# Ordering the last expert blocks by row, results in rows per batch row, and a combine beside them

## The chip, the cores and the metric

The kernel runs on one core of one Trainium2 chip. The metric is the device time of one execution in microseconds (us), as the median of several runs. All data are 32-bit floats.

## The reference

There are B = 4 rows of T = 512 tokens with C = 512 channels. Each row goes through two layers. In each of the four parts a gate computed from side inputs and from x itself comes first, and the part's result is added to x.

```python
x = x + mamba2(gate(x, ...), ...)                 # layer 0, state space model (SSM)
x = x + experts(gate(x, ...), gate_w, gate_b, w1, b1, w2, b2)
x = x + attention(gate(x, ...), w_q, w_kv, w_dense)   # causal, 16 heads, 4 groups
x = x + ffn(gate(x, ...), ...)

def gate(r, k, v, w, u, time_emb):       # scans over the tokens, both ways
    ...
    base = sigmoid(r) * (num / maximum(den, 1e-08))
    return base * (0.8 + 0.2 * tf)

def experts(hidden, ...):                # 8 experts, the best 2 for each token
    logits = x @ gate_w.T + gate_b
    top_vals, top_idx = top_k(logits, 2)
    routing = softmax(top_vals)
    for e in range(8):
        h = x @ w1[e].T + b1[e]
        y = h[:, 0::2] * sigmoid(1.702 * h[:, 0::2]) * (h[:, 1::2] + 1.0)
        ye = y @ w2[e].T + b2[e]
        out = out + ye * sum(routing * (top_idx == e))
```

The change lies in the experts' part and at its border to the attention. Only `sigmoid(r)` of a gate depends on x; the scans, `num` and `den` do not, and are made beside other work.

## The kernel before, in words

**Experts.** Each token has two picks, so there are 4096 picks. They are sorted by expert into blocks of P = 128, where a block holds one expert's picks only; NBLK = 39 blocks always suffice, and those at the end that no pick needs run as dummies. The gated activations of all tokens lie in DRAM as `rows_h`, one row for each token (stored in `logits`, L486). A block gathers its 128 rows with an indirect DMA on POOL (`fetch`, L683, three ahead), turns them with four transposes (`flip`, pfl L695, copied to hT by ACT L697), and runs one round:

- `first_half`: the product pg with the gate half of w1 (L724), g on DVE (L729), a tanh on ACT; then the product pn with the linear half (L735) and two DVE steps to u (L742).
- `finish`: u is turned by four transposes, pyt (L748), and scaled into yT by ACT (L750).
- `down`: the product po with w2 (L757), o on DVE (L762), and an indirect DMA on POOL (L763) that scatters the 128 rows of o into `rows_o`, one row for each pick.

In `round()` for block i, in program order: pg of i, po of i-2, the turn pfl of i+1, pn of i, and `finish` of i-1. The scheduler of the language decides the order on each engine from this, and may move an instruction ahead of others; `after(engine)` (L83) forbids what stands under it to be placed before the last instruction that the engine has so far.

**Two parts.** The first NEARLY = 17 blocks hold picks of rows 0 to 2 and run beside the SSM of row 3. When row 3 is routed (`route` L488: counts by matmuls pcnt, offsets on DVE L553, token numbers by ptok L555), `order_blocks(NEARLY, NBLK)` (L588) ranks the blocks that are left, by a matmul with a lower triangle (pidx L603), and makes for each place the list of rows to gather (`idx_h`), of rows to scatter to (`idx_o`) and its expert (`eb`). The id of a pick (`res_id`, L436) is its row in `rows_o`: 1 + 2048 for a second pick + the token's number over all rows; row 0 is for dummies. idx_h comes from it by an addition and a mask. The blocks stand in the order of the experts, whatever their row.

Weights go on SP's queue (`weights`, `load_w1` L657, `load_w2` L668). The first 17 blocks have one slot of weights; from block 17 on there are two, taken in turn, and a slot is loaded only when its expert changes.

**Border to the attention.** `combine(b)` (L1351) takes a row's results back: for each of four tiles of 128 tokens two loads of 128 x 512 on SP's queue (rr L1359), a scaling on ACT (L1361), a scaled sum on DVE (L1362), four transposes on PE (pcb L1367) and an addition to x on DVE (L1371). A load must come after every scatter to `rows_o` that could touch the same rows, and a scatter can touch all of them. Then `gated` loads what is made of the gate for the attention (1 MB, SP), takes tanh of x on ACT and multiplies on DVE. The attention starts with the keys pk (L1435) and values pv (L1443) of row 0, group 0. Rows 1 to 3 are combined beside the heads of the row before.

The gates' scans and divisions, which need no x, are a generator that `pump()` takes one step at a time; `more()` (L1378) does so after every round. The two parts meet here:

```python
        order_blocks(NEARLY, NBLK)
        moe.know(NBLK)
        more(NBLK - 8)
        first_group = load_group(0)
        more(NBLK)
        moe.round()
        moe.round()
```

Of the kernel before, what the change touches and what calls it, by code (L numbers as in the profile page):

```python
# [31 lines left out]
TOPK = 2  # L32
# [4 lines left out]
NROW = B * T * TOPK + 1  # L37

NEARLY = -(-((B - 1) * T * TOPK - E * (P - 1)) // P)

HEADS, GROUPS, KVC = 16, 4, 128
HPG = HEADS // GROUPS
# [36 lines left out]
def block_kernel(ctx: ExitStack, tc: tile.TileContext, a: dict, out: bass.AP):  # L79
# [61 lines left out]
    def ps_tp(name):  # L141
        return ps.tile([P, 512], F32, tag="tp", name=name, bufs=2)
# [316 lines left out]
    def logits(h, b, lg, t0, nt):  # L459

        pl = ps_tp("pl")
        for t in range(nt):
            for k in range(NC):
                nc.tensor.matmul(
                    pl[:, t * E : (t + 1) * E],
                    lhsT=h[:, k, t * P : (t + 1) * P],
                    rhs=gw[:, k, :],
                    start=(k == 0),
                    stop=(k == NC - 1),
                )  # L470
        nc.vector.tensor_tensor(
            lg[:, t0 : t0 + nt, :],
            pl[:, : nt * E].rearrange("p (t e) -> p t e", e=E),
            row("gate_b").unsqueeze(1).to_broadcast([P, nt, E]),
            ALU.add,
        )
        for t in range(nt):
            ph_ = ps_tp("pht")
            for k in range(NC):
                nc.tensor.transpose(  # L480
                    ph_[:, k * P : (k + 1) * P], h[:, k, t * P : (t + 1) * P], ident
                )
# [107 lines left out]
    def order_blocks(lo, hi):  # L590

        n = hi - lo
        cv = rt.tile([P, 1], F32, tag="cv", name="cv")
        nc.vector.tensor_tensor(jk, sel, cnt[:, (N2 if lo else N2 - NT), :], ALU.mult)
        nc.vector.tensor_reduce(cv, jk, AX.X, ALU.add)
        use = rt.tile([P, 1], F32, tag="use", name="use")
        if lo == 0:
            nc.vector.scalar_tensor_tensor(use, v_lo, float(P), cv, ALU.add, ALU.is_le)
        else:
            nc.vector.tensor_tensor(use, v_lo, cv, ALU.is_lt)  # L600
            nc.vector.tensor_tensor(use, use, taken, ALU.subtract)
        pi = ps_tp("pidx")
        nc.tensor.matmul(pi[:, P : P + 1], lhsT=tri_lt, rhs=use, start=True, stop=True)  # L603
        rank = rt.tile([P, 1], F32, tag="vrank", name="vrank")
        nc.vector.tensor_copy(rank, pi[:, P : P + 1])
# [8 lines left out]
        nc.vector.tensor_scalar(gf[:, :n], pi[:, :n], B * T - 1.0, None, ALU.add)  # L614
        nc.vector.tensor_copy(idx_h[:, lo:hi], gf[:, :n])
        nc.vector.tensor_scalar(idx_h[:, lo:hi], idx_h[:, lo:hi], B * T - 1, None, ALU.bitwise_and)
        ef = tmp.tile([1, NBLK], F32, tag="th", name="ef")
        nc.vector.tensor_scalar(ef[:, :n], pi[0:1, 2 * P : 2 * P + n], E - 1.0, None, ALU.add)
        nc.vector.tensor_copy(eb[:, lo:hi], ef[:, :n])
        nc.vector.tensor_copy(idx_o[:, lo:hi], pi[:, :n])  # L620

    class Experts:
# [130 lines left out]
        def down(self, i):  # L753
            s, yT = self.reg[i][0], self.yT.pop(i)
            po = ps_acc("po")
            for j in range(NI):
                nc.tensor.matmul(  # L757
                    po, lhsT=yT[:, j, :], rhs=self.w2[s][:, j, :],
                    start=(j == 0), stop=(j == NI - 1)
                )  # L760
# [16 lines left out]
        def round(self):  # L777
# [558 lines left out]
    def load_group(g):  # L1336
# [11 lines left out]
            )  # L1348
        return wq, wkv

    def combine(b):  # L1351

        for t in range(NT):
            bt = b * NT + t
            rr = []
            for c in range(2):
                r = cb.tile([P, C], F32, tag=f"rr{c}", name=f"rr{c}", bufs=2 - c)
                lo = 1 + c * B * T + bt * P
                nc.sync.dma_start(out=r, in_=rows_o[lo : lo + P, :])  # L1359
                rr.append(r)  # L1360
            nc.scalar.mul(rr[0], rr[0], g1[:, bt : bt + 1])  # L1361
            nc.vector.scalar_tensor_tensor(  # L1362
                rr[0], rr[1], g2[:, bt : bt + 1], rr[0], ALU.mult, ALU.add
            )
            pt = ps_tp("pcb")
            for k in range(NC):
                nc.tensor.transpose(  # L1367
                    pt[:, k * P : (k + 1) * P], rr[0][:, k * P : (k + 1) * P], ident
                )
            xs = x[b][:, :, t * P : (t + 1) * P]  # L1370
            nc.vector.tensor_tensor(xs, xs, pt.rearrange("p (k t) -> p k t", t=P), ALU.add)  # L1371

    with tc.tile_pool(name="moe_w2", bufs=1, reuse_waits="tile") as wm:
        moe.add_slot(wm)
# [26 lines left out]
    with att as ph:  # L1401
# [15 lines left out]
            )  # L1417
            return wd

        hs = [None] * B  # L1420

        class Group:
            pass
# [255 lines left out]
```

## Time and profile before

| | us |
| --- | --- |
| runs | 2666.9, 2674.48, 2674.92 |
| median | 2674.48 |
| the profiled execution, own time | 2663.89 |
| its span on the core | 2662.2 |
| mean granted TensorE clock | 0.978 |

The profile names five engines: PE (matmul), PEld (its weight loads), DVE (vector), ACT (scalar), POOL and SP (here they mainly issue DMAs). By stretches of the span, busy time in us and the DMA engines' mean share:

| stretch | what runs | PE | DVE | ACT | POOL | clock | DMA |
| --- | --- | --- | --- | --- | --- | --- | --- |
| 500 to 830 | SSM of row 3, experts' first blocks beside it | 311.9 | 199.9 | 131.6 | 80.8 | 0.95 | 0.26 |
| 830 to 960 | last of the first 17 blocks, counting of row 3 | 120.3 | 68.1 | 38.8 | 22.3 | 0.99 | 0.52 |
| 960 to 1215 | blocks 17 to 38 | 250.2 | 148.5 | 79.0 | 44.2 | 1.00 | 0.83 |
| 1215 to 1260 | combine of row 0, its gate | 14.7 | 11.8 | 8.4 | 1.0 | 0.62 | 0.62 |
| 1260 to 1900 | attention | 620.8 | 375.2 | 302.2 | 0.0 | 0.99 | 0.15 |

A busy time close to the stretch's length says that the engine has no gaps there; PE is that engine nearly everywhere, except from 1215 to 1260. The last scatter is issued at 1219.77 and lands at 1222.94; the first result tile is asked for at 1223.59, and pk starts at 1251.0. The granted clock is that of PE, 1 being full speed.

### The profile page before, as it was taken

The numbers are of one execution on the slowest core, as the hardware profiler recorded it, in microseconds if no ns is written. First come the engines' busy times: TensorE is split into PE (matmuls) and PEld (weight loads), VectorE is DVE, ScalarE is ACT, GpSimd is POOL, SyncE is SP. The second block draws the span as 40 slices with busy tenths as digits, with TensorE's granted clock in tenths as the row PEclk, the third lists the DMA queues.
The fourth block names the chain that finished last, engine by engine and source line by source line (L and its number), as shares of the span: only waits on it lengthen the run. The fifth ranks groups of instructions, "written<-read, shape, count | busy, mean of one in ns | idle before, by whom it ended". The sixth has DMA issues, their size and how long they took to land.

```text
span 2662.2 us, 24889 instructions
## 1 busy us (share of the span) xinstructions
PE 2505.3 (94%) x8398; PEld 1330.1 (50%) x8398; DVE 1432.2 (54%) x2777; ACT 1003.3 (38%) x2044; POOL 284.7 (11%) x403
## 2 busy tenths in 40 slices
PE   3999999999998999995999999999999999999999
PEld 1555555646644444442555555555555554444444
DVE  8888888886524565553675555555454441010110
ACT  4556646455321233331554544444444341000000
POOL 1141322322311111110000000000000000000000
PEclk9989999899998999997999999999999999999999
DMA  6121412213134487875121201111000003000000
GB/s 211 44 70 56 133 44 83 92 56 127 41 128 168 170 313 301 333 303 191 56 87 28 63 29 36 44 44 32 16 9 33 23 27 120 16 0 16 8 8 16
DMA packets 86111, 237.95 MB, mean 89 GB/s; under 512 B 9184, under 2 KB 18528, under 8 KB 75872
## 3 DMA queue, kind: packets, MB, share of 16 engines
q1 hardware_dynamic: 77440, 211.71, 22.9%
q0 software_dynamic: 6240, 20.45, 2.1%
q10 hardware_dynamic: 2304, 4.20, 0.4%
q8 instruction: 67, 1.10, 0.2%
q14 instruction: 60, 0.49, 0.1%
HBM read 268.05 MB, written 46.92 MB: 118 GB/s over the span
## 4 chain that ended last, share of the span: by engine, by line
PE 46%; DVE 4%; ACT 2%; DMA 1%; issue 1%; SPq 0%; POOLq 0%; ACTq 0%; DVEq 0%
PE pd L1521 8%; PE pq L1457 7%; PE pfu L1588 6%; PE pfo L1598 6%; PE pfg L1583 6%; PE pctx L1506 5%; PE psc L1474 3%; PE pv L1443 2%; PE ptp L1497 2%; PE pk L1435 2%; DMA rr<-rows_o 1%; DVE nmax L1479 1%; ACT pr L1484 1%; DVE psc L1477 0%; DVE den L260 0%
## 5 line engine op out<-in xcount | busy, mean ns | idle before, releaser
L1457 PE MATMUL pq<-h,wq 128*128 128x512 f32 x512 | 248.9, 603 | 7.5 <-ACT pr L1484 7.4
L1521 PE MATMUL pd<-cx,wd 128*128 128x512 f32 x512 | 222.4, 593 | 0.0
L923 PE MATMUL pc<-h,wxb 128*128 128x512 f32 x320 | 143.2, 605 | 38.1 <-DVE h L1199 38.1
L1593 DVE SCALAR_TENSOR_TENSOR hd<-pfu,cols,hd 128x512 f32<-128x512 f32 x44 | 33.1, 751 | 269.3 <-PE pfu L1588 269.2
L1592 ACT ACTIVATE hd<-pfg,cols 128x512 f32<-128x512 f32 x44 | 30.2, 687 | 381.0 <-PE pfg L1583 381.0
L1484 ACT ACTIVATE pr<-psc,nmax 128x128 f32<-128x128 f32 (+3 forms) x256 | 135.1, 529 | 98.2 <-DVE nmax L1479 97.3
L1477 DVE TENSOR_TENSOR psc<-psc,mask 128x128 f32<-128x128 f32 x256 | 71.9, 288 | 186.2 <-PE psc L1474 186.2
L1506 PE MATMUL pctx<-pT,v 128*128 128x512 f32 (+3 forms) x512 | 153.4, 443 | 7.3 <-ACT pT L1500 3.9
L1588 PE MATMUL pfu<-h,ffu 128*128 128x512 f32 x352 | 158.7, 593 | 1.0 <-DMA ffu<-in_upT 1.0
L1583 PE MATMUL pfg<-h,ffg 128*128 128x512 f32 x352 | 158.6, 593 | 0.0
L1521 PEld LDWEIGHTS pd<-cx,wd 128*128 128x128 f32 x512 | 96.2, 190 | 114.6 <-issue 110.6
L1474 PE MATMUL psc<-kT,qT 128*128 128x128 f32 (+3 forms) x512 | 151.4, 435 | 0.9 <-ACT pr L1484 0.7
L1598 PE MATMUL pfo<-hd,ffd 128*128 128x512 f32 x352 | 151.7, 592 | 0.0
L724 PE MATMUL pg<-w,hT 128*128 128x512 f32 x312 | 143.7, 602 | 2.0 <-DMA w<-in_w1x 2.0
L757 PE MATMUL po<-w,yT 128*128 128x512 f32 x312 | 142.5, 598 | 2.7 <-ACT yT L750 2.1
L1506 PEld LDWEIGHTS pctx<-pT,v 128*128 128x128 f32 x512 | 93.7, 191 | 97.5 <-issue 35.8
L735 PE MATMUL pn<-w,hT 128*128 128x512 f32 x312 | 140.3, 593 | 0.0
L1529 DVE TENSOR_TENSOR xr<-xr,pd 128x512 f32<-128x512 f32 x64 | 44.0, 688 | 175.5 <-PE pd L1521 175.5
L1479 DVE TENSOR_REDUCE nmax<-psc 128x1 f32<-128x128 f32 (+3 forms) x256 | 123.8, 486 | 2.7
L1457 PEld LDWEIGHTS pq<-h,wq 128*128 128x128 f32 x512 | 87.8, 193 | 65.9 <-issue 57.4
L1497 PEld LDWEIGHTS ptp<-ident,pr 128*128 128x128 f32 x640 | 77.3, 142 | 85.3 <-issue 39.0
L994 PE MATMUL pz<-wzt,h 128*128 128x512 f32 x256 | 119.1, 606 | 0.0
(292 smaller groups left out, 4297.6 us busy)
## 6 DMA issues: line engine op xcount, KB each, us to landing
w<-in_w1x SPq DMA_DIRECT2D x80, 1024.0 KB
w<-in_w2x SPq DMA_DIRECT2D x40, 1024.0 KB
wb<-in_b1x SPq DMA_DIRECT2D x40, 512.0 KB
kt<-in_fT SPq DMA_DIRECT2D x62, 256.0 KB
ek<-ek SPq DMA_DIRECT2D x62, 256.0 KB
ekv<-ekv SPq DMA_DIRECT2D x62, 256.0 KB
g<-num SPq DMA_DIRECT2D x30, 512.0 KB
h<-g SPq DMA_DIRECT2D x11, 1024.0 KB
```

The source lines that it names most:

```text
L724: nc.tensor.matmul(pg, lhsT=hT[:, k, :], rhs=self.w1[s][0][:, k, :], start=(k == 0), stop=(k == NC - 1))
L757: nc.tensor.matmul(po, lhsT=yT[:, j, :], rhs=self.w2[s][:, j, :], start=(j == 0), stop=(j == NI - 1))
L923: nc.tensor.matmul(pc, lhsT=wxb[:, k, m * P : (m + 1) * P], rhs=h[:, k, :], start=(k == 0), stop=(k == NC - 1),)
L1457: nc.tensor.matmul(pq, lhsT=u.wq[:, k, i * KVC : (i + 1) * KVC], rhs=u.h[:, k, :], start=(k == 0), stop=(k == NC - 1),)
L1474: nc.tensor.matmul(psc[:, :n], lhsT=qT[:, qi * P : n], rhs=u.kT[:, :n], start=True, stop=True)
L1479: nc.vector.tensor_reduce(nmax, psc[:, :n], AX.X, ALU.max, negate=True)
L1484: nc.scalar.activation(pr, psc[:, :n], AF.Exp, bias=nmax, accum_out=rsum)
L1506: nc.tensor.matmul(pctx[:, kj * P :], lhsT=u.v[:, kj, :], rhs=pT[:, kj, kj * P :], start=(kj == 0), stop=(kj == NT - 1),)
L1521: nc.tensor.matmul(po, lhsT=u.wd[:, i, m * P : (m + 1) * P], rhs=u.ctxT[i], start=(i == 0), stop=(i == HPG - 1),)
L1583: nc.tensor.matmul(pg, lhsT=wg[:, k, cs], rhs=h[:, k, :], start=(k == 0), stop=(k == NC - 1))
L1588: nc.tensor.matmul(pu, lhsT=wu[:, k, cs], rhs=h[:, k, :], start=(k == 0), stop=(k == NC - 1))
L1598: nc.tensor.matmul(po, lhsT=wdn[:, i, m * P : (m + 1) * P], rhs=hd[i], start=(i == 0), stop=(i == NFF - 1),)
```

## The change

The change has four pieces.

- **Rows of their own.** The ids of the picks are arranged so that each row of the batch has 1024 result rows in one piece: rows 3, 1, 2, 0 of the batch in this order (`AT`), so row 0's results are the last 1024 of `rows_o`. `rows_h` takes the same order of rows, and `idx_h` comes from the id by a mask, a shift and two exclusive ors.
- **Order of the last blocks.** Among the blocks from 17 on, those with picks of row 0 come first, each kind still in the order of experts. At most FIRST = 15 blocks can be of the first kind, so from block 32 on no block holds a pick of row 0, and its scatter is given `rows_o` without the last 1024 rows.
- **Combine of row 0 beside the last blocks.** `combine` is split into `load_results` and `add_results`. Row 0's results are loaded on POOL's queue from block 34's round on, and added tile by tile between the rounds of the last blocks; so is the gate of row 0 (`early_h`, held in a tile of wq's), ahead of the last two `down`. A copy of it for the other groups is made by a DMA on SP.
- **`finish` under `after(nc.tensor)`**: pyt of block i-1 may no longer be placed ahead of pn of block i.

```diff
+FIRST = (T * TOPK + E * (P - 1)) // P
...
+    AT = (TOPK * T) * np.array([B - 1, *range(1, B - 1), 0])
...
-    res_id = [count(f"res{c}", [[P, B * NT]], 1, 1 + c * B * T) for c in range(2)]
+    res_id = [count(f"res{c}", [[TOPK * T, B], [P, NT]], 1, 1 + c * T) for c in range(2)]
+    for r in res_id:
+        for b in (0, B - 1):
+            rb = r[:, b * NT : (b + 1) * NT]
+            nc.vector.tensor_scalar(rb, rb, float(AT[b] - b * TOPK * T), None, ALU.add)
...
-            lo = b * T + (t0 + t) * P
+            lo = (B - 1) * T - int(AT[b]) // TOPK + (t0 + t) * P
...
+        else:
+
+            two = rt.tile([P, 2], F32, tag="two", name="two")
+            nc.vector.tensor_tensor(jk, sel, cnt[:, NT, :], ALU.mult)
+            nc.vector.tensor_reduce(rank, jk, AX.X, ALU.add)
+            nc.vector.tensor_scalar(two[:, 0:1], v_lo, rank, use, ALU.is_lt, ALU.mult)
+            nc.vector.tensor_tensor(two[:, 1:2], use, two[:, 0:1], ALU.subtract)
+            nc.tensor.matmul(pi[:, P : P + 2], lhsT=tri_lt, rhs=two, start=True, stop=True)
+            nc.tensor.matmul(pi[:, P + 2 : P + 3], lhsT=ones, rhs=two[:, 0:1], start=True, stop=True)
...
-        nc.vector.tensor_scalar(idx_h[:, lo:hi], idx_h[:, lo:hi], B * T - 1, None, ALU.bitwise_and)
+        low = tmp.tile([P, NBLK], I32, tag="th", name="low")
+        nc.vector.tensor_scalar(
+            low[:, :n], idx_h[:, lo:hi], T - 1, (B - 1) * T, ALU.bitwise_and, ALU.bitwise_xor
+        )
+        nc.vector.tensor_scalar(
+            idx_h[:, lo:hi], idx_h[:, lo:hi], 1, (B - 1) * T,
+            ALU.logical_shift_right, ALU.bitwise_and,
+        )
+        nc.vector.tensor_tensor(idx_h[:, lo:hi], idx_h[:, lo:hi], low[:, :n], ALU.bitwise_xor)
...
-                out=rows_o[:, :],
+                out=rows_o[: NROW - (TOPK * T if i >= NEARLY + FIRST else 0), :],
...
-                self.yT[i - 1] = self.finish(self.y.pop(i - 1))
+                with after(nc.tensor):
+                    self.yT[i - 1] = self.finish(self.y.pop(i - 1))
...
+    def load_results(b, t, queue):
+
+        rr = []
+        for c in range(2):
+            r = cb.tile([P, C], F32, tag=f"rr{c}", name=f"rr{c}", bufs=2)
+            lo = 1 + int(AT[b]) + c * T + t * P
+            queue.dma_start(out=r, in_=rows_o[lo : lo + P, :])
+            rr.append(r)
+        return rr
...
     def combine(b):
 
         for t in range(NT):
...
+            add_results(b, t, load_results(b, t, nc.sync))
...
         first_group = load_group(0)
-        more(NBLK)
+
+        more(min(NEARLY + FIRST + 2, NBLK - NT - 1))
+        results = {t: load_results(0, t, nc.gpsimd) for t in range(2)}
+        more(moe.i + 1)
+        for t in range(NT):
+            more(moe.i + 1)
+            with after(nc.tensor, nc.vector, nc.scalar):
+                add_results(0, t, results.pop(t))
+            if t + 2 < NT:
+                results[t + 2] = load_results(0, t + 2, nc.gpsimd)
+        assert moe.i == NBLK
+        early_h = gated(2, 0, x[0], wa, tag="wq", name="h2_0")
         moe.round()
         moe.round()
...
-        hs = [None] * B
+        hs = [gp.tile([P, NC, T], F32, tag="h", name="h2")] + [None] * (B - 1)
+        nc.sync.dma_start(out=hs[0], in_=early_h)
...
-            if g == 0 and b == 0:
-                combine(b)
-                hs[b] = gated(2, b, x[b], gp, tag="h", name=f"h2_{b}")
-            u.h = h = hs[b]
+            u.h = h = early_h if (g, b) == (0, 0) else hs[b]
```

`add_results` holds the four steps of the old `combine` behind its loads, unchanged. In `order_blocks` the rank of a block of the second kind is its count among its kind plus the number of those of the first kind; the first call, for the 17 early blocks, ranks as before.

More of the change, by code (lines that the diff above doesn't have):

```diff
@@ L602, in order_blocks @@
         pi = ps_tp("pidx")
-        nc.tensor.matmul(pi[:, P : P + 1], lhsT=tri_lt, rhs=use, start=True, stop=True)
         rank = rt.tile([P, 1], F32, tag="vrank", name="vrank")
-        nc.vector.tensor_copy(rank, pi[:, P : P + 1])
+        if lo == 0:
+            nc.tensor.matmul(pi[:, P : P + 1], lhsT=tri_lt, rhs=use, start=True, stop=True)
+            nc.vector.tensor_copy(rank, pi[:, P : P + 1])
+        else:
[7 more added lines that the diff above has]
+            nc.vector.tensor_scalar(
+                rank, pi[:, P + 1 : P + 2], pi[:, P + 2 : P + 3], two[:, 1:2], ALU.add, ALU.mult
+            )
+            nc.vector.scalar_tensor_tensor(
+                rank, pi[:, P : P + 1], two[:, 0:1], rank, ALU.mult, ALU.add
+            )
         if lo == 0:
@@ L613, in order_blocks @@
         gf = tmp.tile([P, NBLK], F32, tag="th", name="gf")
-        nc.vector.tensor_scalar(gf[:, :n], pi[:, :n], B * T - 1.0, None, ALU.add)
+        nc.vector.tensor_scalar(gf[:, :n], pi[:, :n], NROW - 2.0, None, ALU.add)
         nc.vector.tensor_copy(idx_h[:, lo:hi], gf[:, :n])
-        nc.vector.tensor_scalar(idx_h[:, lo:hi], idx_h[:, lo:hi], B * T - 1, None, ALU.bitwise_and)
+        low = tmp.tile([P, NBLK], I32, tag="th", name="low")
+        nc.vector.tensor_scalar(
+            low[:, :n], idx_h[:, lo:hi], T - 1, (B - 1) * T, ALU.bitwise_and, ALU.bitwise_xor
+        )
+        nc.vector.tensor_scalar(
+            idx_h[:, lo:hi], idx_h[:, lo:hi], 1, (B - 1) * T,
+            ALU.logical_shift_right, ALU.bitwise_and,
+        )
+        nc.vector.tensor_tensor(idx_h[:, lo:hi], idx_h[:, lo:hi], low[:, :n], ALU.bitwise_xor)
         ef = tmp.tile([1, NBLK], F32, tag="th", name="ef")
@@ L1349, in load_group, with add_results @@
         return wq, wkv
+    def load_results(b, t, queue):
[6 more added lines that the diff above has]
+        return rr
+    def add_results(b, t, rr):
+        bt = b * NT + t
+        nc.scalar.mul(rr[0], rr[0], g1[:, bt : bt + 1])
+        nc.vector.scalar_tensor_tensor(
+            rr[0], rr[1], g2[:, bt : bt + 1], rr[0], ALU.mult, ALU.add
+        )
+        pt = ps_tp("pcb")
+        for k in range(NC):
+            nc.tensor.transpose(
+                pt[:, k * P : (k + 1) * P], rr[0][:, k * P : (k + 1) * P], ident
+            )
+        xs = x[b][:, :, t * P : (t + 1) * P]
+        nc.vector.tensor_tensor(xs, xs, pt.rearrange("p (k t) -> p k t", t=P), ALU.add)
     def combine(b):
         for t in range(NT):
[L1354 to L1371, printed above, removed]
+            add_results(b, t, load_results(b, t, nc.sync))
     with tc.tile_pool(name="moe_w2", bufs=1, reuse_waits="tile") as wm:
```

## The prediction

> **What bounds the kernel now.** I read the page's busy row first: PE is busy 2505.3 of 2662.2 us (94%), and the chain of waits that ended last is PE nearly throughout. So the program is a string of matmuls, and a change is worth what it takes out of PE's gaps, less what it adds. The next view is the list of PE's waits, asked for by stretch: 790 to 830, 830 to 960, 960 to 1215 and 1215 to 1260 us. Each row names who waited, for whom, the sum, how often, and the longest.
>
> ```profile
> PE ptok L555 <- DVE os L553: 2.9, 1, 2.9
> ...
> PE pyt L748 <- DVE u L742: 9.4, 6, 1.6
> ...
> PE po L757 <- ACT yT L750: 2.1, 4, 1.2
> ...
> PE pcb L1367 <- DVE rr L1362: 30.3, 5, 15.5
> ```
>
> The reader is to see four costs: the router's counting of the last row, the turn of a block's activations (pyt) issued too early, the down product (po) issued too soon after that turn, and the big one, the combine of row 0 after the last block. PE's timeline shows the last as it stands (start, duration, in brackets the idle time before it and what ended it):
>
> ```profile
> 1206.52 3.60 PE L757 MATMUL po<-w,yT 128*128 128x512 f32 x8
> 1209.95 0.60 PE L748 MATMUL pyt<-ident,u 128*128 128x128 f32 x4
> 1211.80 3.70 PE L757 MATMUL po<-w,yT 128*128 128x512 f32 x8 [1.25 <-ACT yT L750]
> 1231.04 1.08 PE L1367 MATMUL pcb<-ident,rr 128*128 128x128 f32 x4 [15.54 <-DVE rr L1362]
> ```
>
> **Units.** Start to start, four f32 products of 512 columns take 3.43 us (pg, pn, po, pk; the trace counts them as x8), four transposes 0.44, sixteen pv 3.57, a full block 3 x 3.43 + 2 x 0.44 = 11.2. I add PE's content and its stalls. The order of instructions on each engine of the changed program I take from its built form; it holds no times.
>
> **Part 1: the hole before the attention.** Before: from the pyt at 1209.95 to the long pv stretch at 1255.78 are 45.8 us. Content: pyt 0.44, po 3.43, five pcb 2.2, pk 3.43, one pv 0.22, together 9.7. So 36.1 us are idle or slow.
>
> After: the built order has the four result tiles' transposes inside blocks 34 to 37 (counted from 0), and pk right behind the last po. Of that stretch I follow PE from the end of block 31's po, with DVE and ACT in their built order.
> - The results' four first loads stand on POOL's queue behind block 31's scatter (landing 2.7 / 6.4 / 8.2 us, min / median / max) and are needed about 39 us later: hidden.
> - Tile 0: its ACT scaling stands behind the gate's three 1024-wide steps and two table loads. These took 1177.44 to 1183.9 with one yT inside, so 5.9 alone, starting 3.5 after pn. pcb is ready 10.9 after that pn; PE needs 9.0 (pyt, a yT wait of 0.9, po, pg, one pn). Stall **1.9**.
> - Tile 1: ACT scales it after a gate step f that waits for a DVE scan, and DVE adds it behind o. Stall **1.5**.
> - Tile 2: DVE has five gate steps between u and o (1197.32 to 1203.07, 5.7 us). The sum is ready 8.7 after pn, PE is there after 5.9. Stall **2.8**.
> - Tile 3: two scans ahead on DVE, **0.7**. Its two loads come behind block 35's scatter on POOL and its ACT scaling stands ahead of the next hT, th and yT, so everyone waits if it is late.
> - The last po waits for its yT, which stands behind two tanh of h on ACT: **1.4**.
> - The yT wait (part 3) in blocks 32 to 37: two of 0.45, four of 0.9 where no pfl lies between: **4.5**.
>
> That is 12.8 for 36.1: a gain of 23.3. Two rules of the Trainium skill speak against it.
>
> *SBUF — State Buffer*, "The 'DVE blocks DMA' trap (SWDGE)": a transfer issued from POOL has its descriptors written by POOL, which a DVE operation can lock out; it advises the SP or ACT queue. The row: POOL's indirect issues took 0.97 at least, 0.98 as median, 2.00 at most, with DVE at work all the while. By *DMA: Bandwidth & Descriptors*, the SWDGE fit, an estimate is 2.0 + 0.26 MB / 436 GB/s = 2.6 us; the nearest row, the POOL scatter, lands after 6.4. Tile 3's loads are issued 51 us after my origin and wanted at about 55. By the page they cost nothing, by the row some 1.5. I take 0.5.
>
> *TensorE: Matmul & The Clock Gate*, Part 1, says the array falls to half rate after an idle window of about 3.4 us. By it none of these stalls costs more than itself. The trace is harsher:
>
> ```profile
> 765.00:770.00 5.00, 2.35 (x12) 2.21 (x12) 1.11 (x5) 0.82 (x3) 0.00 (x0) 0.51 0.42 130
> 810.00:815.00 5.00, 2.41 (x11) 2.41 (x12) 2.99 (x16) 0.40 (x1) 0.00 (x0) 0.50 0.35 116
> 840.00:845.00 5.00, 5.00 (x13) 2.28 (x12) 1.96 (x3) 0.63 (x1) 1.00 (x1) 1.00 0.03 11
> ```
>
> The third number from the right is the granted clock: 0.51 after an idle of 4.55, 0.50 after one of 2.88, 1.00 among single idles of 1.5. So tile 2's 2.8 may also slow what follows, by about 3 us in the second of these rows; I take 1.
>
> Then row 1's combine, hidden before behind row 0's: its loads wait for the last scatter and queue behind the copy of h (1 MB) and two w_dense tiles (1 MB each). At 400 GB/s they land some 10 us after h is done; PE has pv, two pq (3.57 + 6.87) before the softmax needs ACT. Cost 1 (bounds 0 and 12, rival 2). **Part 1: +21.**
>
> **Part 2: pyt behind pn, up to block 16.** `after(nc.tensor)` puts finish(i-1) behind pn(i).
>
> ```profile
> 842.14 3.60 PE L735 MATMUL pn<-w,hT 128*128 128x512 f32 x8
> 847.25 0.66 PE L748 MATMUL pyt<-ident,u 128*128 128x128 f32 x4 [1.51 <-DVE u L742]
> ```
>
> Here the scheduler had put a block's own pyt right behind its pn, so PE waited for u: 847.25 - 842.14 - 3.43 = 1.68, six times, 10.1. After, the pyt there is that of the block before, and its u is a round old; its po follows 3.4 us of pg later, so no wait. What is late next are weights: one slot, and w1 must arrive between two pg in 7.8 us instead of 9.4. There are three changes of expert in this stretch; about 0.5 each, 1.5. Gain 8.6 (bounds 4 and 10).
>
> The built order also puts a whole block of products between the counting matmuls and ptok. Before, pyt, ptok and ptok waited 0.9, 3.1 and 1.3 from 807.6 to 816.7, and the slow clock to 822 cost some 3 (four transposes 0.9, eight ptok 1.9, eight pg 4.05): 8.4. After, about 0.7. Gain 7.7. The block order's matmul pidx now waits behind two scans on DVE, about 2.6; before, its 0.9 and a slow pg of 4.96 cost about the same: 0. The new arithmetic on res_id, two and idx_h is some twenty DVE operations of 0.15 to 0.3, all under PE's work but four in the start-up: 0.3 lost. **Part 2: +16.**
>
> **Part 3: the same edit from block 22 on.** There the built order is pyt, pfl, po, so po waits for the yT of the pyt just ahead. The trace of before has it in three rounds:
>
> ```profile
> 988.29 0.60 PE L748 MATMUL pyt<-ident,u 128*128 128x128 f32 x4
> 988.72 0.60 PE L695 MATMUL pfl<-ident,hb 128*128 128x128 f32 x4
> 989.57 1.99 PE L757 MATMUL po<-w,yT 128*128 128x512 f32 x4 [0.25 <-ACT yT L750]
> ```
>
> Each costs 989.57 - 988.72 - 0.44 = 0.41 to 0.48. Blocks up to 31 add eleven such: 11 x 0.45 = **-5.0**. Where an f stands ahead on ACT the row at 1211.80 has 1.25.
>
> **Part 4: the new order of the last blocks.** From the reference's inputs the experts get 445, 1766, 393, 17, 483, 772, 163 and 57 picks. Before, blocks 17 to 36 went by expert; after, experts 3, 5, 6, 7 come first (row 0's), then the rest. By the rule that a slot reloads only when its expert changes, 15 loads become 16, and a run of seven in a row becomes two of six. DMA ran at a share of 1.02 from 1036 to 1104 us, with 1.8 us of PE waits for w1 there: **-0.5**. The scatters, gathers and their bytes stay.
>
> **Sum.** 21 + 16 - 5 - 0.5 = 31.5. The profiled execution took 2663.9 (span 2662.2), so 2632 in its terms. The median of the three runs shown is 2674.5, 10.6 above; the prediction is for such a median: **about 2642**, from 2674.5 - 31.5 = 2643 and a little for the runs' low end. Within 0.3% (8 us) is about what a measurement of this kernel cannot tell from no change.
>
> **Rivals.**
> 1. *The yT wait is larger.* If ACT is mostly occupied when pyt ends, each of about 20 late rounds costs the 1.25 of the last row, not 0.45: 16 more, gain 15.5, **2659**. For it: the gates' work still shares ACT. Against: three rounds of the same order show 0.25 to 0.31. Chance 0.17.
> 2. *The exposed combine moves to row 1.* ACT's order has row 1's scalings between the softmax exponents, so a late load stops every head. The row-0 chain took 27 us from 1223.6 to 1250.1; PE has 15 us of work ahead. 12 lost, gain 19.5, **2655**. Chance 0.15.
> 3. *Slower: the forced pyt order.* The same place as rival 1, but ACT is held for long stretches, in each late round by a gate step that waits for DVE or by a result tile not landed. From a cost of (31.5 + 9) / 20 = 2.0 us per round it eats everything; with the 3.1 us of the longest DVE wait in the counting stretch instead, 20 x 2.65 = 53 more, **2696**. For it: yT, hT, th, f and the results' scalings are one ACT queue. Against: in the built order f and th stand ahead of yT but their inputs come 2 to 3 us earlier. Chance 0.07.
> 4. *It doesn't do what it says*, the loads still wait for the last scatter: only parts 2 and 3 remain, gain 10.5, **2664**. The built order has the loads between scatters 31 and 32, so 0.03.
>
> My case keeps 0.58. The range reaches to rivals 1 and 2, and on the other side to a gain of 45 to 55 (no new stalls, the run at the low end): **2619 to 2662**. Chances: faster by over 0.3% 0.88, within 0.04, slower 0.08.
>
> **What would show it.** After: no PE wait of 15 us at pcb, pk within 1 us of the last po; pcb stalls of 1 to 3 in the last blocks; no pyt waits for u between 830 and 930; po waits for yT of 0.2 to 0.4 in some fifteen rounds; the clock 1.00 through the stage change. Wrong it would be if yT waits summed to over 20, if softmax rows waited for rr loads by over 10, or if w1 waits passed 5.

## The result and the profile after

The changed kernel took 2652.44 us (median of 6 runs, 2645.88 to 2657.18), the kernel before 2672.32 (median of 6). The ratio is **0.9933, with a 95% interval of 0.9921 to 0.9945**: 18 us faster, between 15 and 21, where 31.5 were forecast. The time is 10 us above the forecast of 2642 and inside its range. The execution that was profiled is the slowest of the six, with a span of 2655.5.

A span of 2655.5 beside 2662.2 is 6.7 us less, not 18. Executions differ ahead of the experts' part already: the last row's counting matmuls (pcnt) start at 818.1 here and at 807.3 before, and in the ten variants of the changed kernel below at anything from 808.0 to 817.9, with much the same waits on PE up to there and a granted clock that dips at different places. So I compare **stretches between two instructions**, from pcnt on, and take the ratio for the whole. What of the 10.8 us is the change's own, the last experiment asks.

PE's waits after, in the same view as before (who waited, for whom, sum, how often, longest), first from 843 to 985 us and, below the dots, from 985 to 1240:

```profile
PE pg L759 <- DMA w<-in_w1x: 2.4, 1, 2.4
...
PE po L792 <- ACT yT L785: 12.4, 21, 5.2
PE pcb L1406 <- DVE rr L1401: 6.1, 4, 2.3
PE pg L759 <- DMA w<-in_w1x: 4.3, 1, 4.3
```

The wait of pyt for u (9.4) is gone from the list, and pcb's 30.3 have become 6.1, in four pieces. In their place stand 12.4 for yT, one of them 5.2 long, and two waits for w1. PE's timeline shows where they fall (start, duration, idle time before in brackets):

```profile
1133.37 5.40 PE L759 MATMUL pg<-w,hT 128*128 128x512 f32 x8 [4.34 <-DMA w<-in_w1x]
...
1155.01 3.70 PE L792 MATMUL po<-w,yT 128*128 128x512 f32 x8 [0.25 <-ACT yT L785]
...
1188.20 0.63 PE L1406 MATMUL pcb<-ident,rr 128*128 128x128 f32 x4 [1.81 <-DVE rr L1401]
...
1198.11 0.66 PE L1406 MATMUL pcb<-ident,rr 128*128 128x128 f32 x4 [1.44 <-DVE rr L1401]
...
1211.74 5.51 PE L792 MATMUL po<-w,yT 128*128 128x512 f32 x8 [5.23 <-ACT yT L785]
...
1220.42 0.63 PE L1406 MATMUL pcb<-ident,rr 128*128 128x128 f32 x4 [2.31 <-DVE rr L1401]
...
1231.61 0.63 PE L1406 MATMUL pcb<-ident,rr 128*128 128x128 f32 x4 [0.58 <-DVE rr L1401]
...
1234.68 3.70 PE L792 MATMUL po<-w,yT 128*128 128x512 f32 x8 [1.15 <-ACT yT L785]
1238.22 1.88 PE L1488 MATMUL pk<-h,wkv 128*128 128x512 f32 x4
```

The four pcb are the four result tiles, now inside the last blocks; pk follows the last po at once. Two lines are dear: the pg at 1133.37 (block 32) waits 4.34 us for its weights, the po at 1211.74 waits 5.23 us for yT, and both then run slowly, 5.40 and 5.51 us where 3.6 is usual.

The stretches, in us ("b20" is the first pg of block 20):

| kernel | pcnt to b20 | b20 to b30 | b30 to b36 | b36 to pk | pk of row 0 to pk of row 3 |
| --- | --- | --- | --- | --- | --- |
| before | 184.0 | 119.7 | 67.1 | 72.8 | 157.8 |
| after | 168.7 | 118.6 | 76.5 | 56.3 | 160.9 |
| gain | 15.3 | 1.1 | -9.4 | 16.5 | -3.1 |

Their sum is 20.4, at the upper end of the ratio's interval of 15 to 21. From pk of row 3 to the end this execution takes 1256.4 us, before 1253.4, though the change leaves that part as it was; the variants below take 1253.1 to 1258.0 for it. With the 10.8 us ahead of pcnt these 3.0 turn the 20.4 into the 6.7 between the two spans. So the early blocks gave what was forecast, the end of the blocks less, and blocks 30 to 36 lost what had not been forecast.

What held the po at 1211.74? The timeline of the other engines, around tile 3:

```profile
1195.77 1.12 SPq L692 DMA_DIRECT2D w<-in_w1x  x2
...
1198.96 1.10 POOL L1393 DMA_DIRECT2D rr<-rows_o  x2
...
1205.91 0.60 PE L783 MATMUL pyt<-ident,u 128*128 128x128 f32 x4
1209.48 0.72 ACT L1400 ACTIVATE rr<-rr,g 128x512 f32<-128x512 f32 x1 [13.69 <-DMA rr<-rows_o]
1210.11 0.57 ACT L732 COPY hT<-pfl 128x512 f32<-128x512 f32 x1
1210.58 0.63 ACT L121 ACTIVATE th<-g 128x512 f32<-128x512 f32 x1
1211.11 0.59 ACT L785 ACTIVATE yT<-pyt 128x512 f32<-128x512 f32 x1
```

Tile 3's two loads are issued at 1198.96, and the scaling at 1209.48 is tile 3's, which ACT has ahead of tile 2's. Three microseconds ahead of them SP had asked for 3.8 MB of weights, those of block 38, a block without picks. The DMA engines moved 370 GB/s from 1200 to 1210; the results came after 10 us, and ACT, whose next instruction was their scaling, could make no hT, th or yT meanwhile. pyt had been done since 1206.5.

### The profile page after: what moved, and what is told of

It reads as the page before. It is cut to its first block, busy times and chain, and to the rows that moved or that the text cites. A ratio compares the mean times of both kernels' runs of the same rounds, so it can differ in the third digit from the quotient of the medians.

```text
span 2655.5 us, 24901 instructions
## 1 busy us (share of the span) xinstructions
PE 2514.2 (95%) x8400; PEld 1332.9 (50%) x8400; DVE 1435.8 (54%) x2792; ACT 1001.8 (38%) x2042; POOL 291.1 (11%) x411
## 3 DMA queue, kind: packets, MB, share of 16 engines
q1 hardware_dynamic: 77152, 214.60, 23.3%
## 4 chain that ended last, share of the span: by engine, by line
PE 72%; DVE 16%; ACT 5%; DMA 4%; issue 2%; POOL 0%; SPq 0%; POOLq 0%; ACTq 0%; DVEq 0%
PE pd L1574 8%; PE pq L1510 6%; PE pfu L1641 6%; PE pfo L1651 6%; PE pfg L1636 6%; PE pctx L1559 5%; PE pn L770 4%; PE pg L759 4%; PE po L792 4%; PE psc L1527 3%; PE pc L959 2%; PE po L1195 2%; PE pz L1030 2%; PE ptp L1550 2%; PE pv L1496 2%
## 5 line engine op out<-in xcount | busy, mean ns | idle before, releaser
L792 PE MATMUL po<-w,yT 128*128 128x512 f32 x312 | 145.0, 606 | 12.4 <-ACT yT L785 12.4
```

What stands on the lines that cost most here:

```text
L792: nc.tensor.matmul(po, lhsT=yT[:, j, :], rhs=self.w2[s][:, j, :], start=(j == 0), stop=(j == NI - 1))
```

## The experiments

Four theories. **A**: the forecast's terms hold, and what is missing before pk is tile 3's loads behind the weights of the empty block, and w1 of block 32. **B** (rival 1): the forced pyt is dearer in every late round. **C** (rival 2): the loss is row 1's combine. **D**, formed last: part of it lies ahead of pcnt. Ratios are to the kernel before, with their 95% interval.

| kernel | ratio | pcnt to b20 | b20 to b30 | b30 to b36 | b36 to pk |
| --- | --- | --- | --- | --- | --- |
| changed | 0.9933 (0.9921 to 0.9945) | 168.7 | 118.6 | 76.5 | 56.3 |
| pyt_alone | 0.997 (0.9957 to 0.9983) | 168.8 | 120.6 | 70.2 | 75.9 |
| pyt_free | 0.9984 (0.9972 to 0.9997) | 183.3 | 116.3 | 73.9 | 60.1 |
| results_early | 0.9914 (0.988 to 0.9947) | 168.9 | 118.6 | 76.6 | 52.2 |
| dummy_expert | 0.9928 (0.9906 to 0.9949) | 170.6 | 118.6 | 77.3 | 54.1 |
| results_on_SP | 0.9947 (0.9926 to 0.9968) | 170.1 | 118.6 | 76.3 | 53.5 |
| group_later | 0.9906 (0.9878 to 0.9934) | 168.8 | 118.6 | 69.3 | 53.9 |
| turn_between | 0.9946 (0.993 to 0.9963) | 168.7 | 117.7 | 73.4 | 57.7 |
| all_four | 0.9879 (0.9859 to 0.9898) | 169.5 | 118.6 | 76.5 | 40.5 |
| three_late | 0.9863 (0.9833 to 0.9893) | 168.9 | 118.6 | 72.5 | 42.3 |
| three_late_turn | 0.9846 (0.9813 to 0.9878) | 169.7 | 118.6 | 72.5 | 40.0 |
| row1_on_POOL | 0.9959 (0.9936 to 0.9981) | 170.9 | 118.6 | 77.3 | 55.8 |
| rows_alone | 1.0021 (1.0009 to 1.0034) | 184.9 | 119.8 | 67.0 | 72.3 |

**The edit on pyt by itself** (pyt_alone: the kernel before with it; pyt_free: the changed kernel without it).

```diff
             if i - 1 in self.y:
-                self.yT[i - 1] = self.finish(self.y.pop(i - 1))
+                with after(nc.tensor):
+                    self.yT[i - 1] = self.finish(self.y.pop(i - 1))
```

> The kernel before with one edit of the change: pyt may not stand ahead of the next block's pn. Theory (parts 2 and 3 of the prediction stand as they are): the counting of row 3 and the early blocks gain about 15 us up to the first product of block 20, as in the trace after; the late blocks lose about 0.5 us each, 5 to 9 in all; the hole before the attention stays. Total 6 to 10 us faster than before (ratio about 0.997), with no pyt wait for u of 1.5 us between 830 and 930. Rival (the 15 us of the trace after come from the new order of blocks or from a lucky clock): within 3 us of before, and the counting matmuls still followed by waits of 3 us.

> The changed kernel without that one edit. Theory: it loses the 15 us of the counting stretch and early blocks and wins back 0.5 us in each of 16 late rounds, so 5 to 8 us slower than the changed kernel, 10 to 13 faster than before (ratio about 0.9955). Its hole before the attention is as short as in the changed kernel: pk within 60 us of block 36's pg. Rival (the edit is what lets the combine stand beside the last blocks): the hole comes back, and it is no faster than before.

pyt_alone came out as expected, 8 us faster. Its first stretch is 168.8, the changed kernel's to a tenth, so the 15 us of that stretch are this edit's alone. It loses 4 us in blocks 20 to 36 and 3 behind. pyt_free was expected 10 to 13 us faster than before and was 4: the hole is short there too (60.1), but blocks 30 to 36 cost 73.9 instead of 67.1, which no theory had. Its waits from 800 to 990 us bring the old rows back:

```profile
PE pyt L783 <- DVE u L777: 9.5, 6, 1.6
PE ptok L564 <- DVE os L562: 2.5, 1, 2.5
```

In blocks 30 to 36 PE waits 5.71 us for block 32's w1 (1138.82, the pg then takes 5.85). So the other three pieces together are worth 4 us (1 to 7), and the one edit on pyt 8 by itself (5 to 11), or 14 of the 18 when it is added last; 8 and 4 make 12 and not 18, which the widths of the intervals allow. B is not wholly wrong: from block 20 to 36 the edit costs 195.1 - 190.2 = 4.9 us, 0.3 for each of 16 rounds on average.

**Tile 3's loads.** Three ways to take the wait away: all eight loads together behind block 31's scatter (results_early), no weights for the empty block (dummy_expert), SP's queue, where the loads stand ahead of those weights (results_on_SP).

```diff
-            r = cb.tile([P, C], F32, tag=f"rr{c}", name=f"rr{c}", bufs=2)
+            if b or t < 2:
+                r = cb.tile([P, C], F32, tag=f"rr{c}", name=f"rr{c}", bufs=2)
+            else:
+                r = wm.tile([P, C], F32, name=f"rr{c}_{t}")
...
-        results = {t: load_results(0, t, nc.gpsimd) for t in range(2)}
+        results = {t: load_results(0, t, nc.gpsimd) for t in range(NT)}
...
-            if t + 2 < NT:
-                results[t + 2] = load_results(0, t + 2, nc.gpsimd)
```

> The changed kernel with all eight result loads of row 0 issued together behind the scatter of block 31, in buffers of their own for tiles 2 and 3. Theory (tile 3's two loads stand behind 3.8 MB of weights in the DMA engines): po's wait of 5.2 us for yT falls to about 0.7, and the po of 5.5 us after it to 3.4: 6 to 7 us less from block 36's pg to pk, 49 to 51 us where it is 56.3. Rival (ACT's own order holds yT there, whatever the loads do): the wait stays above 3 us, the stretch above 54.

```diff
-    nc.vector.tensor_scalar(v_e, v_e, 1.0 / NQ, 1.0 - E, ALU.mult, ALU.add)
+    nc.vector.tensor_scalar(v_e, v_e, 1.0 / NQ, 2.0 - E, ALU.mult, ALU.add)
...
-        nc.vector.tensor_scalar(ef[:, :n], pi[0:1, 2 * P : 2 * P + n], E - 1.0, None, ALU.add)
+        nc.vector.tensor_scalar(ef[:, :n], pi[0:1, 2 * P : 2 * P + n], E - 2.0, None, ALU.add)
```

> The changed kernel in which blocks without picks name expert 6 instead of 7. With these picks the last block then finds its weights in place, so 3.8 MB of weights are not loaded while tile 3's results are; nothing else moves. Theory (the weights of a block that holds no picks are what tile 3's loads wait for): the results land 3 to 5 us after issue instead of 9.4, po's wait for yT there falls to about 0.7, and the stretch from block 36's pg to pk to 49 to 51 us. Rival (loads from POOL's queue are late of themselves, DVE being at work): landing stays at 8 us or more, the stretch above 54.

```diff
-        results = {t: load_results(0, t, nc.gpsimd) for t in range(2)}
+        results = {t: load_results(0, t, nc.sync) for t in range(2)}
...
-                results[t + 2] = load_results(0, t + 2, nc.gpsimd)
+                results[t + 2] = load_results(0, t + 2, nc.sync)
```

> The changed kernel with row 0's result loads on SP's queue instead of POOL's. There tile 3's loads stand ahead of the last block's weights, and the first four stand ahead of block 36's w1 and wait for the scatter of block 31. Theory (which queue counts only through what stands ahead in it): tile 3 lands within 5 us of its issue, po's wait for yT of 5.2 us falls to about 0.7, and nothing else waits, as two blocks lie between: from block 36's pg to pk 50 to 53 us. Rival (a wait on SP holds up all weights behind it): w1 waits of 3 us or more in blocks 36 to 38, the stretch 56 us or more.

The long wait went in all three: po's wait for yT there is 0.69 in results_early, in results_on_SP there is none for yT (0.95 for w2), and dummy_expert has

```profile
1203.07 3.70 PE L792 MATMUL po<-w,yT 128*128 128x512 f32 x8 [1.69 <-ACT yT L785]
```

dummy_expert fell between its two sides. The slowest result load landed after 6.3 us, above the 3 to 5 of the theory and below the 8 of the rival, on the same queue as in the changed kernel, where it took 9.9. So the 3.8 MB of weights are worth 3.6 us of the landing and 3.5 us of po's wait (5.23 - 1.69); why 6.3 remain was not tried.

results_on_SP missed in the landing. Tile 3's loads do stand ahead of block 38's weights there, but behind those of block 37, asked for from 1182.58 on, and three transfers of a gate. SP's and ACT's lines:

```profile
1188.93 2.73 SPq L1393 DMA_DIRECT2D rr<-rows_o  x2
...
1196.51 0.60 ACT L785 ACTIVATE yT<-pyt 128x512 f32<-128x512 f32 x1 [1.59 <-PE pyt L783]
...
1200.37 0.72 ACT L1400 ACTIVATE rr<-rr,g 128x512 f32<-128x512 f32 x1 [3.26 <-DMA rr<-rows_o]
```

ACT still waits for the first of them 11.4 us after its issue, and not the 5 that were expected. But in this kernel ACT has the same hT, th and yT ahead of tile 3's scaling, so PE does not wait for it. The wait of 5.23 thus took two things: loads that land late with the weights in the DMA engines, and a scaling that stands ahead of yT on ACT.

The stretch to pk, though, fell by 2.2 to 4.1 and not by 6 to 7. PE's timeline of results_early says why:

```profile
1206.58 3.70 PE L792 MATMUL po<-w,yT 128*128 128x512 f32 x8 [0.69 <-ACT yT L785]
1210.12 1.02 PE L759 MATMUL pg<-w,hT 128*128 128x512 f32 x2
1214.07 0.63 PE L1409 MATMUL pcb<-ident,rr 128*128 128x128 f32 x4 [2.93 <-DVE rr L1404]
1214.53 4.44 PE L759 MATMUL pg<-w,hT 128*128 128x512 f32 x6
```

PE now meets the next wait, tile 2's pcb behind the gate's steps on DVE, 2.93 us where it was 2.31; and the six pg behind it take 4.44 where 2.74 is usual. The same stretch by windows (stretch, its length, busy PE, PEld, DVE, ACT and POOL with counts, then granted clock, DMA share, GB/s) has the clock at 0.59:

```profile
1214.00:1218.00 4.00, 3.93 (x9) 1.96 (x10) 0.69 (x1) 0.00 (x0) 0.77 (x1) 0.59 0.99 280
```

dummy_expert has it worse, 4.11 us at that pcb. Its stretch of 54.1 lies at the rival's edge. None of the three ratios is apart from the changed kernel's: a gain of 3 us is within their intervals.

**w1 of block 32.** The attention's first weights, 1.5 MB on SP, are asked for after block 30. By the picks of these inputs, blocks 30 to 33 kept their slot's expert in the order before and loaded nothing. In the new order blocks 27 to 32 each change it, so the 1.5 MB fall into a row of loads.

```diff
-        more(NBLK - 8)
-        first_group = load_group(0)
-
         more(min(NEARLY + FIRST + 2, NBLK - NT - 1))
+        first_group = load_group(0)
```

> The changed kernel with the attention's first weights (wq and wkv, 1.5 MB on SP) asked for after block 33 instead of after block 30. Theory (block 32's w1 waits 4.3 us because these 1.5 MB stand ahead of it on SP): that wait falls below 0.5 and the slow pg after it to 3.4, so the stretch from block 30's pg to block 36's takes 70 to 71 us where it takes 76.5 in the changed kernel; about 6 us less in all. Rival (six blocks in a row that each load 3.8 MB are too much by themselves): the wait stays above 3 us, the stretch above 75.

Blocks 30 to 36 took 69.3 us where they took 76.5, and from 985 us to pk no wait for w1 is left. That is A; the ratio is 7 us better than the changed kernel's, though the two intervals overlap.

**pyt ahead of pn**, so that a whole product lies between pyt and po, from block 18 on.

```diff
                 self.flip(i + 1)
+            if i > NEARLY and i - 1 in self.y:
+                with after(nc.tensor):
+                    self.yT[i - 1] = self.finish(self.y.pop(i - 1))
+            if i < NBLK:
                 self.y[i] = next(half)
```

> The changed kernel with pyt of block i-1 asked for ahead of pn of block i instead of behind it, from block 18 on; the built order is then pyt, pfl, pg, pn, po. Theory (each late round loses 0.5 us because po follows pyt with only pfl between): all po waits for yT of 0.25 and 0.69 go, blocks 20 to 36 take 187 to 189 us where they take 195.1, and the whole is 6 to 8 us faster than the changed kernel. Rival (weights, 3.8 MB in 11.2 us, set the pace once PE is faster): w1 waits grow by what the yT waits lose, gain under 3 us.

The waits of 0.25 went, and blocks 20 to 36 took 191.1 us instead of 195.1 (187 to 189 expected); the ratio is not better. Block 32 comes to its weights sooner and waits 4.74 for them, and then runs at 6.35 (the 1.5 MB stay ahead of them in this kernel). Tile 0's pcb waits 3.21, its scaling standing behind the gate's steps on ACT and DVE. What PE saves, these hand back: a mixed outcome, between theory and rival.

**All together.** all_four takes the edits of results_early, group_later and turn_between, and moves four of the gates' steps (pump) out of the rounds of the last blocks:

```diff
-        def more(limit):
+        def more(limit, steps=1):
...
-                with after(nc.vector):
-                    pump()
+                for _ in range(steps):
+                    with after(nc.vector):
+                        pump()
...
+        more(NBLK - 10)
-        more(min(NEARLY + FIRST + 2, NBLK - NT - 1))
+        more(min(NEARLY + FIRST + 2, NBLK - NT - 1), 2)
...
-            more(moe.i + 1)
+            more(moe.i + 1, 0)
```

> The changed kernel with pyt ahead of pn from block 18 on, all results loaded at once, the attention's first weights after block 33, and four of the gates' steps taken from the rounds of blocks 35 to 38 into those of blocks 29 to 33. If the terms add: 6 to 8 (pyt), 6 (w1 of block 32), 4 (tile 3) and 2 to 4 (tile 2's stall of 2.3 and the slow clock after it) make it 18 to 22 us faster than the changed kernel, a ratio to before of 0.985 to 0.987, with no wait over 1.5 us between block 20 and pk. Rival (the weights or DVE take over): w1 or pcb waits of over 3 us, and a gain of 8 or less.

It gained 14 us on the changed kernel, not 18 to 22. The end is short, 40.5, but blocks 20 to 36 took 195.1 again: two steps in a round make pyt wait for u (1.55 and 2.05), since in this order u is young, and w1 waits add 5.7. three_late therefore leaves pyt where the change has it and puts the double steps into the rounds of blocks 31 to 34 (`more(NBLK - 8)`, then `more(34, 2)`, `more(moe.i + 1, 2)`); three_late_turn adds pyt ahead of pn for the last three blocks (`i > NBLK - 4`).

> The changed kernel with pyt where the change has it, all results loaded at once, the attention's first weights after block 33, and the gates' steps of the rounds of blocks 35 to 38 taken into those of blocks 31 to 34, which load no weights. If the cause of the 8 us missing before pk is what the single runs say (w1 of block 32, tile 3's loads, tile 2 behind the gates' steps on DVE), blocks 30 to 36 take 69 to 71 us (76.5 in the changed kernel), the stretch from there to pk 42 to 46 (56.3), and the whole is 16 to 19 us faster than the changed kernel: ratio to before 0.986 to 0.988. Rival (the steps only move their stalls to blocks 31 to 34): those blocks take 4 us or more longer, and the gain is 12 or less.

> The same with pyt ahead of pn in the last three blocks alone, so that po there has a product between. Theory: the three waits of 0.69 and part of the 1.15 before the last po go, 2 us less than the run beside it from block 36's pg to pk, nothing elsewhere. Rival (pyt then waits for u or for ACT in the same rounds): no difference, within 1 us.

Both did as expected from block 36 to pk (42.3 and 40.0) and in the ratio; blocks 30 to 36 took 72.5, 1.5 over the forecast, 1.4 of it one wait for w1. (The expectation has blocks 31 to 34 load no weights; by the picks that holds for 33 and 34 alone.) What is left for PE to wait for in three_late_turn from 985 to 1255 us:

```profile
PE po L792 <- ACT yT L785: 5.4, 17, 0.7
PE pq L1515 <- ACT pr L1542: 2.0, 1, 2.0
PE pg L759 <- DMA w<-in_w1x: 1.4, 1, 1.4
PE pctx L1564 <- ACT pT L1558: 1.1, 1, 1.1
PE pcb L1413 <- DVE rr L1408: 0.5, 1, 0.5
```

It runs in 2628.72 us (median of 6), 1.5% under the kernel before (0.9846), where the changed kernel has 0.67%: it beats both.

**Row 1's combine.** In the changed kernel the stretch from pk of row 0 to pk of row 2 is 5.6 us longer than before, and the next, to pk of row 3, gives 2.5 back.

```diff
-            add_results(b, t, load_results(b, t, nc.sync))
+            add_results(b, t, load_results(b, t, nc.gpsimd if b == 1 else nc.sync))
```

> The changed kernel with row 1's eight result loads on POOL's queue, which is empty there, instead of SP's, where they stand behind the copy of h and two dense weights (3 MB). In the changed kernel pk of row 0 to pk of row 2 takes 98.6 us, before 93.1 (row 3 gives 2.6 back). Theory (row 1's combine is slow because DVE holds its adds, the gates' steps and the softmax's maxima in one queue; ACT waits only 0.8 us for a load): within 1.5 us of 98.6. Rival 2 of the prediction (the loads are late on SP): 3 us or more less, 95.5 or below, and pq's wait of 2.0 for pr gone.

Neither came. From pk of row 0 to pk of row 1 took 49.6 us where it took 38.3. The timeline of this run:

```profile
1256.69 0.72 ACT L1400 ACTIVATE rr<-rr,g 128x512 f32<-128x512 f32 x1 [2.98 <-DMA rr<-rows_o]
1257.32 1.06 ACT L1518 ACTIVATE qT<-pq 128x512 f32<-128x512 f32 x2
...
1257.95 4.63 PE L1527 MATMUL psc<-kT,qT 128*128 128x128 f32 x8 [6.82 <-ACT qT L1518]
```

On POOL the loads are issued from 1245.7 on, behind the copy of h and two dense weights and beside row 1's gate, and land after up to 11.4 us. ACT waits for them with the queries behind it, and PE waits 6.8 us for qT. That is rival 2's mechanism to the letter, called up by the experiment. The same place in the changed kernel:

```profile
1262.78 0.37 ACT L1537 ACTIVATE pr<-psc,nmax 128x128 f32<-128x128 f32 x1 [3.57 <-DVE nmax L1532]
1263.29 3.70 PE L1510 MATMUL pq<-h,wq 128*128 128x512 f32 x8 [2.03 <-ACT pr L1537]
...
1265.43 0.72 ACT L1400 ACTIVATE rr<-rr,g 128x512 f32<-128x512 f32 x1 [0.80 <-DMA rr<-rows_o]
```

There a load is late by 0.8 us at most; PE waits 2.0 for pr, and pr waits for the maximum on DVE, which has two results' sums and additions to x just ahead of it. That the queue on DVE is the whole of the 3 us was read from this row and not tried.

**The rows of their own, alone**, on the kernel before: `AT`, the arithmetic on res_id, the store in `logits`, idx_h, and the loads of `combine`, as in the diff of the change. Order, combine and pyt stay as before.

```diff
+    res_id = [count(f"res{c}", [[TOPK * T, B], [P, NT]], 1, 1 + c * T) for c in range(2)]
+    for r in res_id:
+        for b in (0, B - 1):
...
+            lo = (B - 1) * T - int(AT[b]) // TOPK + (t0 + t) * P
...
+                lo = 1 + int(AT[b]) + c * T + t * P
```

> The kernel before with the first piece of the change alone: result rows in one piece for each batch row, and the arithmetic on res_id and idx_h that goes with it; order of blocks, combine and pyt as before. Theory (the forecast's 0.3 us for this arithmetic): first pz at 81.6 to 83.5, pcnt of row 3 below 808.5, the whole within 2 us of before. Rival (this arithmetic moves DVE's order in the start-up, one pc product falls behind pdt, and PE stalls and runs slowly there): first pz at 84 to 87 as in all profiles of the changed kernel, 2 to 4 us slower than before (ratio 1.001 to 1.0015); from pcnt on nothing differs from before by more than 2 us.

The rival was right: a ratio of 1.0021, 5.6 us slower (2.4 to 9), where it said 2 to 4. From pcnt on it stands within 1 us of before in every stretch; the loss lies ahead. Its PE timeline from the start of the first row's SSM:

```profile
42.06 35.35 PE L936 MATMUL pc<-h,wxb 128*128 128x512 f32 x76 [38.73 <-DVE h L1212]
77.76 3.85 PE L883 MATMUL pdt<-wxb,h 128*128 128x16 f32 x32 [0.35 <-DVE xc L951]
81.46 3.52 PE L936 MATMUL pc<-h,wxb 128*128 128x512 f32 x4
84.81 5.74 PE L1007 MATMUL pz<-wzt,h 128*128 128x512 f32 x13
```

and that of the kernel before:

```profile
41.36 35.50 PE L923 MATMUL pc<-h,wxb 128*128 128x512 f32 x78 [38.08 <-DVE h L1199]
77.06 3.72 PE L870 MATMUL pdt<-wxb,h 128*128 128x16 f32 x32 [0.21 <-DVE xc L938]
80.63 1.11 PE L923 MATMUL pc<-h,wxb 128*128 128x512 f32 x2
81.57 7.03 PE L994 MATMUL pz<-wzt,h 128*128 128x512 f32 x16
```

The first pc comes 0.7 us later, and one more product (x2) stands behind pdt. Behind pdt, two products (x4) take 3.35 us from start to start where one took 0.94; the one moved accounts for 0.9, and some 1.5 us are lost to a granted clock of 0.67 from 82 to 86. The first pz starts at 84.3 to 86.6 in all twelve profiles with this piece, and at 81.6 and 83.0 in the two without: 3.3 us between the means, 1.3 at the least. In the changed kernel's own profile pz is 5.0 us late, of the 10.8 at pcnt; the rest is not traced to the change. Whether the other 2 to 3 us of the ratio here are real its interval doesn't say.

## Why the prediction was right, and where it was not

The time came within 10 us of the forecast, but the gain is 18 where 31.5 were forecast, outside the ratio's 15 to 21. The time lies in the range because the range reached up to rivals 1 and 2, and neither took the 12 to 16 us that it was drawn for. That the time lies in it is in part luck, so the account goes term by term.

**The start-up: mis-sized.** 0.3 was forecast, from four DVE operations by their durations. That new operations also move the order of others was in the built order and not asked for; the first pz is some 3 us later, and the piece alone costs 5.6 (2.4 to 9).

**Part 2, the early blocks: right.** 16.3 was forecast for the counting and the blocks up to 16 (8.6 + 7.7); the stretch gained 15.3, and pyt_alone shows that the one edit makes it. The weights were named as what is late next, at 1.5; they cost 2.4 + 0.3.

**Part 1, tiles 0 to 2 and the last po: right in mechanism and size.** Forecast 1.9, 1.5, 2.8, 0.7 for the pcb and 1.4 for the last yT; measured 1.81, 1.44, 2.31, 0.58 and 1.15. Each came from counting what stands ahead in ACT's and DVE's queue, with durations from other rows.

**Part 1, tile 3's loads: the term that failed.** I took 0.5, having looked only at which queue issues them and how fast a transfer from POOL lands; the outer bound of 1.5 was the same 6.4 us landing. I had noted that hT, th and yT stand behind this scaling, but not asked what else is in the DMA engines then. It cost 5.23 for yT, where 1.4 was in the sum (the 0.5 and the usual 0.9), and 1.9 of slow po (5.51 - 3.60), where 1 was: 4.7 us too much. *SBUF — State Buffer*, "The 'DVE blocks DMA' trap (SWDGE)", in the Trainium skill, warned of this queue for another reason, a lock by DVE. These traces don't show that: the issues took 0.54 to 0.58 us each with DVE busy, and the same loads on the same queue landed in 6.3 once the weights were gone. On SP, the queue that it advises, the first was still awaited after 11.4; PE's wait went there by ACT's order alone.

**Part 4, the order of the last blocks: mis-sized, with the wrong reason.** Forecast -0.5, from 15 loads against 16. What counts is where the row of loads meets the 1.5 MB (group_later): 4.34 us and a slow pg of 1.8 more, 6.1. The new order also gives something back that I had not seen, 3.4 us in blocks 20 to 30 (119.7 before, 116.3 in pyt_free), where the order before, by the picks, had seven loads in a row; that this is the reason was not tried.

**Part 3: right.** A late round takes 11.69 us instead of 11.18 (start to start of pg in blocks 33 to 35, after and before): 0.51 where 0.45 was taken (over blocks 20 to 36 it is 0.3 against pyt_free, whose rounds have other stalls).

**Row 1: mis-sized.** 1 was forecast, for late loads; it cost 3.1, and by the row above at DVE, which was not tried.

From block 20 to pk 16.3 was forecast (23.3 - 0.5 - 1 - 5.0 - 0.5) and 8.2 measured; 4.7 + (6.1 - 0.5) - 3.4 = 6.9 of the 8.1 between them is named. With 2.1 at row 1 and 1.0 in the early blocks the 8.1 are the way from 31.5 to 20.4 behind pcnt; the start-up takes it on towards the 18 of the ratio. Rivals 1 and 3 fell (no late round costs 1.25 except at tile 3); rival 2 has the right place and not the reason; rival 4 fell with the first pcb.

Of the signs that were named, pk right behind the last po, the short pcb, the missing waits of pyt and the po waits of 0.25 (in sixteen rounds) came. Two did not: the clock was 0.50 from 1211 to 1215 us, not 1.00 through the stage change, and the waits for w1 summed to 6.8 us (2.4 and 4.3, shown above), past the 5 that were named as a sign of being wrong; 4.3 of them are where part 4 failed.

## What to carry to other kernels

When a transfer is moved earlier, list what every other queue has in the DMA engines at that moment, and what stands behind its first reader: a 0.5 MB load behind 3.8 MB of weights took 10 us although it came from another queue (6.3 without them), and with it held hT, th and yT. When blocks are put in another order, look for fixed requests in the schedule that lay where the old order had room. And of a change with several pieces, run each alone: here one line that only forbids an early placement gave 8 us by itself, and the other three pieces together 4.

## What the runs showed of the hardware

Over the 4 us behind an idle time of PE the granted clock was 1.00 after 2.31 and 2.41 us, 0.59 after 2.93, 0.57 after 4.34 and 0.54 after 5.23, so that each of the last three stalls cost 1.7 to 1.9 us more than itself. By *TensorE: Matmul & The Clock Gate*, Part 1, in the Trainium skill, an idle window of about 3.4 us is what it takes; 2.93 was enough here, while 3.42 us in turn_between, some 4 us after a slow stretch, left the clock at 1.00. A rule in idle time alone doesn't describe these rows. The clock also differs between executions: late in the attention, from 1885.4 before and from 1876.0 after, the same row's heads took 60.4 us at a clock of 1.00 in one and 61.9 at 0.97 in the other, with the same two waits of 2.5 and 0.2 us.
